# Four graph-attention layers on one core: gathers of two layers wait for earlier scores, range checks once per layer

## The chip, the cores and the metric

The kernel runs on one core of a Trainium2 chip. The metric is the device time of one execution in microseconds (us), median of several runs. A core has five engines that work side by side, each through its own queue in order: PE (TensorE, matrix products), DVE (VectorE), ACT (ScalarE), POOL (GpSimd) and SP (SyncE, which here only issues DMAs). Engines wait for each other through semaphores. An instruction whose semaphore has not been counted up yet holds everything behind it in its own queue.

## The reference, cut to what matters

```python
# x: (8, 2048, 64), adj: (2048, 2048) of 0/1, sparse
# --- layer 0 ---
h = relu(layernorm(x));  x = x + attention(h, h, adj)        # dot-product scores
# --- layer 1 ---
h = relu(layernorm(x)) @ W1
e = leaky_relu((h @ a1)[:, :, None] + (h @ a2)[:, None, :])  # additive scores
x = x + elu(softmax(where(adj > 0, e, -inf)) @ h)
# --- layer 2 ---  four heads of dot-product attention, then one more on the result
x = x + layernorm(leaky_relu(gat(leaky_relu(gat(relu(layernorm(x)), 4 heads)) @ Wo)))
# --- layer 3 ---  as layer 1 with relu for elu and weights W3
x = x + relu(softmax(...) @ h)
```

The graph is sparse, with a few nodes of high degree among the first ones. So a softmax over a row needs only the neighbours' rows, and the kernel gathers these instead of multiplying whole 2048 x 2048 matrices.

## The kernel before

**Tiles and slots.** The 2048 nodes are 16 tiles of 128. A row of a node holds all 8 batches (8 x 64 = 512 numbers). Tile i takes `ROWS[i] + PACKED[i]` slots; a slot is one gathered row for each of the 128 partitions. The tiles need 17, 8, 6, 5, 5, 5, 4, 4, 4, 4, 4, 3, 3, 3, 3, 3 slots, 81 in all, tile 0 by far the most. `gather` (L246) issues one indirect DMA per slot from POOL's queue (L253), from the layer's table in DRAM into `ring`, an SBUF buffer of 26 slots that all tiles share in turn. A slot is 2048 bytes per partition in layer 0 and layer 2, and 2080 in layers 1 and 3, whose rows carry eight additive terms (`F + B` columns).

**Stages.** `pipeline` (L214) writes the stages of all tiles one after the other: in step n it writes the last stage for tile n-s first and `take`, the gathers of the n-th tile of the layer's order, last. The program is built under `schedule_with_timeline_sim=True` (L1436): the order of instructions on each engine is fixed when the program is built, by when they become ready in a simulated time, so it isn't exactly the order of the loops.

**Layers 1 and 3** come from one function, `additive(k, ...)` (L500), with k = 1 and k = 4 (the number of the table). Its stages:

- `take`: the gathers.
- `sums` (k = 4 only): exponentials of the gathered terms (L507, ACT), their sum `S` (L510), its largest and smallest value per tile into `most` and `least` (L511, L512), an estimate `z` of the row's largest score (L515, L517), and a pair `fs`: a copy of `f1s` made on ACT (L519) and the leaky value of z (L448, called from L520).
- `first`: the scores `s` (L532, L535), leaky (L448, called from L536), the exponentials `w` (L542), copied to `wp` (L544).
- `check`: `second` (L455) adds up the weights (`by_query`, L459), inverts them (L460) and forms the weighted sum of the gathered rows: products on DVE (L380), added up on PE (L385). For k = 1 the largest and smallest `rec` per tile are noted (L550, L551).
- `third`, `project`: division (L465), transposition (L306, L307), product with the weights (L561), then `elu_add` (L567, layer 1) or `relu_add` (L905, layer 3).
- In layer 1 alone: layer norm (L267 to L298, with the power `ln_r` L290 on POOL) and `products` (L321) for layer 2.

In layer 1 POOL thus issues gathers and computes `ln_r` for tiles that are some steps further on. In layer 3 it issues gathers only.

**Range checks.** `most` and `least` hold one column per check and tile. At the end (L912 to L927) they are compared with 1e30 and 1e-30, and with other checks give `flag`; if it is set, a slow dense version runs instead. Layer 2's first attention notes `most[:, 2]` (L808), its second `most[:, 4]` in `second3` (L877, reduction L882).

Of the kernel before, what the change touches and what calls it, by code (L numbers as in the profile page):

```python
# [1 line left out]

# [6 lines left out]
F32 = mybir.dt.float32  # L9
# [4 lines left out]
OP = mybir.AluOpType  # L14
AX = mybir.AxisListType

P = 128
NEG = -1.0e30
SLOPE = 0.2
# [15 lines left out]

PAIRS = [0, 0, 2, 2, 2, 0, 0, 0, 2, 2, 2, 2, 2, 2, 2, 2]
QE = 4


MAKING = [15, 14, 13, 0, 12, 11, 10, 1, 9, 2, 8, 3, 7, 4, 6, 5]  # L40
# [19 lines left out]
def edge_stack(ctx: ExitStack, tc: tile.TileContext, x_in, adj, w1, w1t, a1, wh, wht, bh, wo, bo,  # L60
# [32 lines left out]
    mba = const.tile([P, NS], F32, name="mba")  # L93
    mbb = const.tile([P, NS], F32, name="mbb")
    nc.gpsimd.memset(mba, 0.0)
    f1s = const.tile([P, NT, B], F32, name="f1s")
    over = const.tile([P, NT, 3], F32, name="over")
    most = const.tile([P, 5, NT], F32, name="most")
    least = const.tile([P, 2, NT], F32, name="least")
    ring = const.tile([P, RING, F + B], F32, name="g")  # L100
    qidx = const.tile([P, sum(PACKED)], I32, name="qidx")
    selt_all = const.tile([P, sum(PACKED), P], F32, name="selt")
# [140 lines left out]
    def row(i, t):  # L243
        return ring[:, (held[i] + t) % RING, :F]

    def gather(k, i, st):  # L246

        n = SLOTS[i]
        assert sum(SLOTS[j] for j in held) + n <= RING
        held[i], front[0] = front[0], (front[0] + n) % RING  # L250
        cols = table[k].shape[1]
        for t in range(n):
            nc.gpsimd.indirect_dma_start(  # L253
                out=ring[:, (held[i] + t) % RING, :cols], out_offset=None, in_=table[k][:, :],
                in_offset=bass.IndirectOffsetOnAxis(ap=idx[:, OFF[i] + t:OFF[i] + t + 1], axis=0))

    def load(st, name, src, bufs):
        st[name] = rows_pool[0].tile([P, F], F32, name=name, bufs=bufs)
# [79 lines left out]
    def pre_d(k, u):  # L338

        def f(i, st):  # L340
            xh = st["xh"]
            if u is not None:
                p = ps_m.tile([P, F], F32, name="m")
                for j in range(F // P):
                    nc.tensor.matmul(p[:, 4 * j:4 * j + 4], st["xt"][:, j, :], u, start=True, stop=True)
                pv = p[:, :2 * B].rearrange("p (b t) -> p t b", t=2)
                nc.scalar.copy(f1s[:, i, :], pv[:, 0, :])
                nc.scalar.copy(xh[:, F:], pv[:, 1, :])
            store_rows(k, i, xh, k != 2)
        return f  # L350
# [94 lines left out]
            nc.vector.tensor_tensor(dst, p, u, op=OP.max)  # L445

    def leaky(dst, src):
        nc.vector.scalar_tensor_tensor(dst, src, SLOPE, src, op0=OP.mult, op1=OP.max)  # L448


    def first0(i, st):
        w = slots(w_all, i)
        exps(i, w, scores(i, st, st["rows"]), mba, D ** -0.5)

    def second(i, st, wp=None):  # L455
        w = slots(w_all, i)
        d, p = by_query(i, w, B)
        st["rec"] = small.tile([P, B], F32, name="rec")
        nc.vector.tensor_tensor(st["rec"], p, d, op=OP.add)  # L459
        nc.vector.reciprocal(st["rec"], st["rec"])  # L460
        st["y"] = weigh_sum(i, st, w) if wp is None else weigh_sum(i, st, wp, eng=nc.vector)
        done(i, st)
# [36 lines left out]

    def additive(k, wd, *finish):  # L500
        def take(i, st):
            gather(k, i, st)

        def sums(i, st):
            w = slots(w_all, i)
            for t, m, g in rows(i, 0, SLOTS[i]):
                nc.scalar.activation(w[:, t:t + m], g[:, :, F:], AF.Exp, scale=1.0 / TEMP)  # L507
            d, p = by_query(i, w, B)
            S = small.tile([P, B], F32, name="S")
            nc.vector.tensor_tensor(S, p, d, op=OP.add)  # L510
# [8 lines left out]
            nc.scalar.copy(st["fs"][:, 0, :], f1s[:, i, :])  # L519
            leaky(st["fs"][:, 1, :], z)  # L520

        def first(i, st):
            K, T = ROWS[i], PACKED[i]
            w = slots(w_all, i)
            s = slots(s_all, i)
            fs = st["fs"].rearrange("p t b -> p (t b)") if k == 4 else f1s[:, i, :]
            n = 2 * B if k == 4 else B
            pr = tiny(2 * B)
            nc.vector.tensor_copy(pr[:, :n], fs)
            pv = by_edge(i, fs, n)  # L530
            for t, m, g in rows(i, 0, K):
                nc.vector.tensor_tensor(s[:, t:t + m, :], g[:, :, F:], pr[:, None, :B].to_broadcast([P, m, B]),  # L532
                                        op=OP.add)
            for t, m, g in rows(i, K, K + T):
                nc.vector.tensor_tensor(s[:, t:t + m, :], g[:, :, F:], pv[:, t - K:t - K + m, :B], op=OP.add)  # L535
            leaky(s, s)  # L536
            if k == 4:
                nc.vector.tensor_tensor(s[:, :K, :], s[:, :K, :], pr[:, None, B:].to_broadcast([P, K, B]),
                                        op=OP.subtract)
                nc.vector.tensor_tensor(s[:, K:, :], s[:, K:, :], pv[:, :, B:], op=OP.subtract)  # L540
                nc.vector.tensor_scalar(s, s, 60.0, None, op0=OP.min)
            nc.scalar.activation(w, s, AF.Exp)  # L542
            wp = tiny((K + T) * B)
            nc.vector.tensor_copy(wp, w.rearrange("p t b -> p (t b)"))  # L544
            st["wp"] = wp.rearrange("p (t b) -> p t b", b=B)

        def check(i, st):
            second(i, st, st["wp"])
            if k == 1:
                nc.vector.tensor_reduce(most[:, 0, i:i + 1], st["rec"], AX.X, OP.max)  # L550
                nc.vector.tensor_reduce(least[:, 0, i:i + 1], st["rec"], AX.X, OP.min)  # L551
# [12 lines left out]
        mid = [sums] if k == 4 else []  # L564
        pipeline(take, *mid, first, both(check, xs_rows), third, project, *finish[1:])
# [14 lines left out]
    with tc.tile_pool(name="rows", bufs=2) as rp:  # L580
# [125 lines left out]
        with tc.tile_pool(name="more", bufs=1) as more_pool[0], psum_pools()[0] as ps_q, psum_pools()[1] as ps_t:  # L706
            bank[0] = ps_t.tile([P, F], F32, name="tiny")
            order[:] = ORDER1
            nc.sync.dma_start(out=sel_dram[:, :], in_=sel_all[0])
            additive(1, wd1, elu_add, pre_b, pre_c(q2), pre_d(2, None), products)  # L710

    with tc.tile_pool(name="l2", bufs=2) as l2p, \
# [88 lines left out]
        def second2(i, st):  # L803
            d, p = by_query(i, st["w"], B * H)
            rec = st["rec"] = small.tile([P, B, H], F32, name="rec2")
            rf = rec.rearrange("p b h -> p (b h)")
            nc.vector.scalar_tensor_tensor(rf, p, 1.0, d, op0=OP.add, op1=OP.add)
            nc.vector.tensor_reduce(most[:, 2, i:i + 1], rf, AX.X, OP.max)  # L808
# [43 lines left out]
    with psum_pools()[0] as ps_q, psum_pools()[1] as ps_t, tc.tile_pool(name="rows2", bufs=2) as rp:  # L852
# [63 lines left out]
        nc.vector.tensor_scalar(ok, most.rearrange("p k i -> p (k i)"), 1e30, None, op0=OP.is_lt)  # L916
        nc.vector.tensor_scalar(ok2, least.rearrange("p k i -> p (k i)"), 1e-30, None, op0=OP.is_gt)
# [522 lines left out]
```

## Time and profile before

| | us |
|---|---|
| median of 3 runs (lowest, highest) | 1672.45 (1670.03, 1676.54) |
| the profiled execution's own time | 1721.51 |
| its span, first to last instruction | 1719.7 |
| busy in the span: PE / DVE / ACT / POOL | 1215.1 / 1318.4 / 744.5 / 1153.4 |
| first gather of layer 1 | 402.51 |
| first gather of layer 2, first attention | 659.58 |
| first gather of layer 2, second attention | 1218.36 |
| first gather of layer 3 | 1529.04 |

By stage, in us (PE, DVE, ACT and POOL: busy time):

| stretch | length | PE | DVE | ACT | POOL | granted TensorE clock |
|---|---|---|---|---|---|---|
| layer 1, 400 to 656 | 256 | 184.81 | 181.59 | 139.71 | 107.28 | 0.89 |
| layer 2 first, 656 to 1218 | 562 | 483.48 | 434.01 | 267.40 | 459.08 | 0.95 |
| layer 2 second, 1218 to 1527 | 309 | 205.48 | 249.17 | 143.78 | 226.97 | 0.76 |
| layer 3, 1527 to 1720 | 193 | 135.70 | 102.71 | 17.92 | 76.90 | 0.83 |

A profile is one execution with a recorder running. The rows of the timeline that follow below give start, duration, engine, line, operation, output and input, shapes, count, and in brackets how long the engine sat idle before it and what ended that. "remote" and "another core or an unknown queue" stand for a semaphore that was counted up at a moment at which no recorded instruction or DMA ended; "issue" for time with no visible cause.

### The profile page before, as it was taken

What the parts mean: (1) busy time and instruction counts of PE and PEld (TensorE: products, weight loads), DVE (VectorE), ACT (ScalarE), POOL (GpSimd) and SP (SyncE); (2) the same over time, 40 slices, a digit from 0 to 9 for tenths busy, and PEclk for the clock granted to TensorE, in tenths of its full rate; (3) what the DMA queues carried; (4) which work ended last, traced back from release to release, by engine and by line L of the source; (5) the groups of instructions that cost most, each with busy time, mean ns of one, the idle gap of its engine ahead of it and who ended that gap; (6) DMA issues with size and microseconds to landing.
All of it is one profiled execution on the core that took longest, in us unless ns stands there. A gap on an engine that the chain in (4) does not pass through costs nothing.

```text
span 1719.7 us, 15784 instructions
## 1 busy us (share of the span) xinstructions
PE 1215.1 (71%) x3771; PEld 606.6 (35%) x3771; DVE 1318.4 (77%) x2748; ACT 744.5 (43%) x2378; POOL 1153.4 (67%) x903
## 2 busy tenths in 40 slices
PE   0025667776479974599997999999467877555877
PEld 0002334443234431234342444443223433333545
DVE  6979999992469987699997899831389889823656
ACT  5841324441146783356531545545234445620011
POOL 5766867786554125898789889985577896654540
PEclk9998876896699997799999999999787879657989
DMA  5555454455566447656255345200643542235651
GB/s 172 167 182 179 152 200 153 141 198 156 147 201 235 158 179 260 233 189 208 87 201 200 113 157 177 87 13 19 255 141 99 154 146 70 81 119 164 197 170 51
DMA packets 85787, 266.94 MB, mean 155 GB/s; under 512 B 14627, under 2 KB 14659, under 8 KB 75446
## 3 DMA queue, kind: packets, MB, share of 16 engines
q0 software_dynamic: 37328, 141.05, 26.7%
q1 hardware_dynamic: 48358, 124.79, 20.4%
q8 instruction: 32, 0.52, 0.1%
q14 instruction: 69, 0.57, 0.1%
HBM read 208.74 MB, written 57.05 MB: 155 GB/s over the span
## 4 chain that ended last, share of the span: by engine, by line
PE 25%; POOL 11%; DVE 9%; issue 7%; ACT 5%; DMA 3%; another core or an unknown queue 2%; DVEq 0%; SPq 0%; POOLq 0%; ACTq 0%
PE y L787 10%; PE y L385 4%; POOL g L253 3%; POOL wh L772 3%; PE m L836 2%; ACT yn L795 2%; PE m L824 2%; PE y L779 2%; POOL wg L380 1%; DMA g<-table,idx 1%; POOL ln_r L290 1%; DMA rows<-table 1%; PE m L399 1%; DVE prod L755 1%
## 5 line engine op out<-in xcount | busy, mean ns | idle before, releaser
L253 POOL DMA_INDIRECT g<-table,idx x405 | 399.2, 986 | 233.5 <-issue 161.7
L772 POOL TENSOR_TENSOR wh<-g,w 128x1024 f32<-128x1024 f32 x162 | 307.5, 1918 | 30.0 <-PE y L787 28.0
L385 PE MATMUL y<-wg,ident 128*128 128x512 f32 x392 | 234.5, 729 | 72.7 <-POOL wg L380 64.3
L290 POOL TENSOR_TENSOR ln_r<-ln_q,mhalf 128x8 f32<-128x8 f32 x80 | 135.8, 1701 | 160.6 <-DVE ln_q L288 85.1
L759 DVE TENSOR_REDUCE s<-prod 128x32 f32<-128x2048 f32 x81 | 184.0, 2286 | 14.8 <-ACT w L761 12.9
L380 POOL TENSOR_TENSOR wg<-g,w 128x1024 f32<-128x1024 f32 (+1 forms) x91 | 158.9, 1756 | 37.3 <-ACT w L436 24.2
L787 PE MATMUL y<-wh,ident 128*128 128x512 f32 x320 | 154.6, 610 | 28.9 <-POOL wh L785 25.1
L385 PE MATMUL y<-wg,selt 128*128 128x512 f32 x256 | 141.6, 663 | 5.4 <-POOL wg L380 4.4
L385 PEld LDWEIGHTS y<-wg,ident 128*128 128x128 f32 x392 | 81.6, 228 | 162.2 <-POOL wg L380 78.9
L787 PE MATMUL y<-wh,selt 128*128 128x512 f32 x256 | 124.7, 614 | 10.4 <-POOL wh L772 10.4
L795 ACT ACTIVATE yn<-y,rec 128x64 f32<-128x64 f32 x512 | 111.2, 368 | 27.5 <-PE y L787 26.9
L755 DVE TENSOR_TENSOR prod<-q,g 128x2048 f32<-128x2048 f32 x49 | 111.5, 2276 | 5.3 <-ACT g L753 4.6
L399 PE MATMUL m<-w,selt 128*128 128x8 f32 (+1 forms) x384 | 59.5, 258 | 76.0 <-ACT w L542 38.2
L380 DVE TENSOR_TENSOR wg<-g,tiny 128x1024 f32<-128x1024 f32 (+1 forms) x92 | 98.2, 1086 | 17.1 <-PE y L385 8.8
L399 PEld LDWEIGHTS m<-w,selt 128*128 128x128 f32 x384 | 63.5, 213 | 122.3 <-ACT w L542 43.6
L442 DVE SCALAR_TENSOR_TENSOR zt<-m,bhc,att 128x512 f32<-128x512 f32 x64 | 47.3, 738 | 75.0 <-ACT att L441 74.4
L298 ACT ACTIVATE xh<-x,ln_r 128x64 f32<-128x64 f32 x256 | 88.3, 428 | 18.8 <-POOL ln_r L292 18.7
L787 PEld LDWEIGHTS y<-wh,ident 128*128 128x128 f32 x320 | 59.0, 193 | 104.9 <-issue 63.8
L428 PE MATMUL q<-rows,sel 128*128 128x512 f32 x128 | 84.3, 762 | 15.7 <-DVE prod L422 5.0
L753 ACT COPY g<-g 128x512 f32<-128x512 f32 x81 | 50.4, 622 | 100.5 <-DVE prod L755 87.9
L755 DVE TENSOR_TENSOR prod<-qe,g 128x2048 f32<-128x2048 f32 x32 | 73.0, 2282 | 17.0 <-DMA qe<-qtab,qidx 15.9
L779 PE MATMUL y<-rows,ident 128*128 128x512 f32 x128 | 70.0, 634 | 18.3 <-DMA rows<-table 13.6
(210 smaller groups left out, 2584.7 us busy)
## 6 DMA issues: line engine op xcount, KB each, us to landing
qtab<-q SPq DMA_DIRECT2D x16, 1040.0 KB
a<-in_adj_dram SPq DMA_DIRECT2D x16, 1024.0 KB
q<-qtab SPq DMA_DIRECT2D x14, 1040.0 KB
table<-xh SPq DMA_DIRECT2D x48, 256.0 KB
rows<-table SPq DMA_DIRECT2D x48, 256.0 KB
xs<-x SPq DMA_DIRECT2D x48, 256.0 KB
x<-xs SPq DMA_DIRECT2D x48, 256.0 KB
table<-xh SPq DMA_DIRECT2D x32, 260.0 KB
```

What stands on the lines that cost most here:

```text
L253: nc.gpsimd.indirect_dma_start(out=ring[:, (held[i] + t) % RING, :cols], out_offset=None, in_=table[k][:, :], in_offset=bass.IndirectOffse ...
L290: nc.gpsimd.tensor_tensor(st["rstd"][:, 0, :], q, mhalf, op=OP.pow)
L298: nc.scalar.activation(dst[:, b * D:(b + 1) * D], st["src"][:, b * D:(b + 1) * D], func, bias=0.0 if st["less"] is None else r[:, 1, b:b + ...
L380: eng.tensor_tensor(wg[:, :m].rearrange("p t (b d) -> p t b d", b=B), g[:, :, :F].rearrange("p t (b d) -> p t b d", b=B), w[:, t0:t0 + m, ...
L385: nc.tensor.matmul(y, lhs(i, t), wg[:, t - t0, :], start=(t == 0 and own is None), stop=(t == n - 1))
L399: nc.tensor.matmul(p[:, :cols], selt(i, t), packed[:, t, :], start=(t == 0), stop=(t == T - 1))
L755: nc.vector.tensor_tensor(pr.rearrange("p (b h) d -> p b h d", h=H), q[:, :B * H * D].rearrange("p (b h d) -> p b h d", h=H, d=D), heads(g ...
L759: nc.vector.tensor_reduce(s[:, t - lo, :], pr, AX.X, OP.add)
L772: nc.gpsimd.tensor_tensor(wg, heads(row(i, t))[:, :, None, :].to_broadcast([P, B, 2, D]), w[:, :, 2 * k:2 * k + 2, None].to_broadcast([P, ...
L779: nc.tensor.matmul(st["ys"][j], ident, xb[:, 4 * j:4 * j + 4], start=True, stop=False)
L787: nc.tensor.matmul(st["ys"][j], lhs(i, t), wg[:, 4 * j:4 * j + 4], start=False, stop=(t == n - 1))
L795: nc.scalar.activation(yn[:, b, h, :], st["ys"][j][:, b, h, :], AF.Copy, scale=st["rec"][:, 4 * j + b, 2 * k + h:2 * k + h + 1])
```

## The change

Three edits, in the order of the title.

1. `gather` takes an instruction `behind`. In `additive`, the first gather of the n-th tile (n >= 3) gets a semaphore wait for the `leaky` of the scores (DVE) of the tile three places ahead in the order. The tile's other gathers carry no such wait themselves.
2. The reductions to `most` and `least` per tile go away in layers 1, 3 and in layer 2's second attention. The values go to `seen`, a buffer with a column per tile, which is reduced once per layer (`bounds`), over 16 x 8 columns. In layer 1 `rec` is itself a part of `seen`. `seen` is used by three layers in turn. Layer 2's first attention keeps its reduction per tile, into `most2`, and gets one more over it.
3. `f1s` gets a second place per tile for the leaky value, so the copy to `fs` on ACT (L519) goes away.

```diff
+SPREAD = 3
...
-    f1s = const.tile([P, NT, B], F32, name="f1s")
+    f1s = const.tile([P, NT, 2, B], F32, name="f1s")
     over = const.tile([P, NT, 3], F32, name="over")
-    most = const.tile([P, 5, NT], F32, name="most")
-    least = const.tile([P, 2, NT], F32, name="least")
+    most = const.tile([P, 5], F32, name="most")
+    least = const.tile([P, 2], F32, name="least")
+    seen = const.tile([P, NT, B], F32, name="seen")
+    most2 = const.tile([P, NT], F32, name="most2")
...
-    def gather(k, i, st):
+    taken = {}
+
+    def gather(k, i, st, behind=None):
...
         for t in range(n):
-            nc.gpsimd.indirect_dma_start(
+            g = nc.gpsimd.indirect_dma_start(
                 out=ring[:, (held[i] + t) % RING, :cols], out_offset=None, in_=table[k][:, :],
                 in_offset=bass.IndirectOffsetOnAxis(ap=idx[:, OFF[i] + t:OFF[i] + t + 1], axis=0))
+            if behind is not None and t == 0:
+                tc.add_manual_dep(g.ins, behind.ins.name, mybir.DependencyInfo(
+                    mybir.DependencyClass.Sync, mybir.DependencyReason.DATA), reason="gather")
...
-                nc.scalar.copy(f1s[:, i, :], pv[:, 0, :])
+                nc.scalar.copy(f1s[:, i, 0, :], pv[:, 0, :])
...
+    def bounds(at, values, low=None):
+
+        nc.vector.tensor_reduce(most[:, at:at + 1], values.rearrange("p i c -> p (i c)"), AX.X, OP.max)
+        if low is not None:
+            nc.vector.tensor_reduce(least[:, low:low + 1], values.rearrange("p i c -> p (i c)"), AX.X, OP.min)
+
-    def second(i, st, wp=None):
+    def second(i, st, wp=None, rec=None):
...
-        st["rec"] = small.tile([P, B], F32, name="rec")
+        st["rec"] = small.tile([P, B], F32, name="rec") if rec is None else rec
...
         def take(i, st):
-            gather(k, i, st)
+            n = order.index(i)
+            gather(k, i, st, taken[k, order[n - SPREAD]] if n >= SPREAD else None)
...
-            S = small.tile([P, B], F32, name="S")
+            S = seen[:, i, :]
             nc.vector.tensor_tensor(S, p, d, op=OP.add)
-            nc.vector.tensor_reduce(most[:, 1, i:i + 1], S, AX.X, OP.max)
-            nc.vector.tensor_reduce(least[:, 1, i:i + 1], S, AX.X, OP.min)
...
-            nc.vector.tensor_tensor(z, z, f1s[:, i, :], op=OP.add)
-            st["fs"] = small.tile([P, 2, B], F32, name="fs")
-            nc.scalar.copy(st["fs"][:, 0, :], f1s[:, i, :])
-            leaky(st["fs"][:, 1, :], z)
+            nc.vector.tensor_tensor(z, z, f1s[:, i, 0, :], op=OP.add)
+            leaky(f1s[:, i, 1, :], z)
...
-            leaky(s, s)
+            taken[k, i] = leaky(s, s)
...
         def check(i, st):
-            second(i, st, st["wp"])
-            if k == 1:
-                nc.vector.tensor_reduce(most[:, 0, i:i + 1], st["rec"], AX.X, OP.max)
-                nc.vector.tensor_reduce(least[:, 0, i:i + 1], st["rec"], AX.X, OP.min)
+            second(i, st, st["wp"], seen[:, i, :] if k == 1 else None)
...
             additive(1, wd1, elu_add, pre_b, pre_c(q2), pre_d(2, None), products)
+            bounds(0, seen, 0)
...
-            nc.vector.scalar_tensor_tensor(rec, p, 1.0, d, op0=OP.add, op1=OP.add)
-            nc.vector.tensor_reduce(most[:, 4, i:i + 1], rec, AX.X, OP.max)
-            nc.vector.reciprocal(rec, rec)
+            nc.vector.scalar_tensor_tensor(seen[:, i, :], p, 1.0, d, op0=OP.add, op1=OP.add)
+            nc.vector.reciprocal(rec, seen[:, i, :])
...
         pipeline(take3, first3, second3, third3, both(pre_b, xs_rows), fourth3, pre_b, pre_c(u3), pre_d(4, u3))
+        bounds(4, seen)
...
         additive(4, wd3, relu_add)
-        nc.vector.memset(most[:, 3, :], 0.0)
-        ok = small.tile([P, 5 * NT], F32, name="ok", bufs=1)
-        ok2 = small.tile([P, 2 * NT], F32, name="ok2", bufs=1)
+        bounds(1, seen, 1)
+        nc.vector.tensor_reduce(most[:, 2:3], most2, AX.X, OP.max)
+        nc.vector.memset(most[:, 3:4], 0.0)
+        ok = small.tile([P, 5], F32, name="ok", bufs=1)
+        ok2 = small.tile([P, 2], F32, name="ok2", bufs=1)
```

More of the change, by code (lines that the diff above doesn't have):

```diff
@@ L1 @@
-from contextlib import ExitStack
+from contextlib import ExitStack, nullcontext
 import concourse.bass as bass
@@ L447, in leaky @@
     def leaky(dst, src):
-        nc.vector.scalar_tensor_tensor(dst, src, SLOPE, src, op0=OP.mult, op1=OP.max)
+        return nc.vector.scalar_tensor_tensor(dst, src, SLOPE, src, op0=OP.mult, op1=OP.max)
     def first0(i, st):
@@ L525, in first @@
             s = slots(s_all, i)
-            fs = st["fs"].rearrange("p t b -> p (t b)") if k == 4 else f1s[:, i, :]
             n = 2 * B if k == 4 else B
+            fs = f1s[:, i].rearrange("p t b -> p (t b)")[:, :n]
             pr = tiny(2 * B)
@@ L807, in second2 @@
             nc.vector.scalar_tensor_tensor(rf, p, 1.0, d, op0=OP.add, op1=OP.add)
-            nc.vector.tensor_reduce(most[:, 2, i:i + 1], rf, AX.X, OP.max)
+            nc.vector.tensor_reduce(most2[:, i:i + 1], rf, AX.X, OP.max)
             nc.vector.reciprocal(rf, rf)
@@ L909, in edge_stack @@
         additive(4, wd3, relu_add)
-        nc.vector.memset(most[:, 3, :], 0.0)
-        ok = small.tile([P, 5 * NT], F32, name="ok", bufs=1)
-        ok2 = small.tile([P, 2 * NT], F32, name="ok2", bufs=1)
+        bounds(1, seen, 1)
[3 more added lines that the diff above has]
+        ok2 = small.tile([P, 2], F32, name="ok2", bufs=1)
         ok3 = small.tile([P, 3 * NT], F32, name="ok3", bufs=1)
-        nc.vector.tensor_scalar(ok, most.rearrange("p k i -> p (k i)"), 1e30, None, op0=OP.is_lt)
-        nc.vector.tensor_scalar(ok2, least.rearrange("p k i -> p (k i)"), 1e-30, None, op0=OP.is_gt)
+        nc.vector.tensor_scalar(ok, most, 1e30, None, op0=OP.is_lt)
+        nc.vector.tensor_scalar(ok2, least, 1e-30, None, op0=OP.is_gt)
         nc.vector.tensor_scalar(ok3, over.rearrange("p i k -> p (i k)"), 0.5, None, op0=OP.is_lt)
```

## The prediction

> **What bounds the kernel now.** I read the page's groups first, then the busy time in stretches of 20 us over layer 1, then the timelines of POOL, DVE and ACT there, and the same for layer 3. The change acts in layers 1 and 3, and a little in layer 2's second attention, so the rest (layer 0 and layer 2's first attention, 960 us) is taken as it is.
>
> Windows of layer 1; columns are the stretch, its length, busy time (and count) of PE, PEld, DVE, ACT and POOL, granted clock, DMA share and GB/s:
>
> ```profile
> 400.00:420.00 20.00, 10.10 (x26) 5.57 (x26) 8.33 (x32) 0.67 (x3) 13.35 (x14) 0.57 0.58 165
> 420.00:440.00 20.00, 5.22 (x26) 3.05 (x24) 2.60 (x11) 0.59 (x1) 15.18 (x16) 0.77 0.75 213
> 440.00:460.00 20.00, 7.48 (x26) 5.36 (x26) 6.97 (x19) 5.42 (x15) 7.59 (x8) 0.54 0.48 132
> ...
> 560.00:580.00 20.00, 19.70 (x74) 10.34 (x74) 20.00 (x42) 16.58 (x47) 1.93 (x3) 1.00 0.35 133
> ```
>
> From about 500 on DVE is the bound (20.00 of 20). From 420 to 460 nothing works but POOL. There it issues gathers one after another, 1.25 us apart (0.95 each and 0.30 between), 35 of them without a break. Timelines of POOL, ACT and DVE:
>
> ```profile
> 445.20 0.95 POOL L253 DMA_INDIRECT g<-table,idx  x1 [0.30 <-issue]
> 455.21 0.95 POOL L253 DMA_INDIRECT g<-table,idx  x1 [9.06 <-DVE wg L380]
> 462.15 1.68 POOL L290 TENSOR_TENSOR ln_r<-ln_q,mhalf 128x8 f32<-128x8 f32 x1 [3.49 <-DVE ln_q L288]
> ```
> ```profile
> 451.10 0.60 ACT L570 ACTIVATE e<-q 128x512 f32<-128x512 f32 x1 [29.48 <-remote]
> ```
> ```profile
> 434.30 0.17 DVE L535 TENSOR_TENSOR s<-g,m 128x16 f32<-128x16 f32 x1 [8.21 <-remote]
> 452.39 0.70 DVE L572 SCALAR_TENSOR_TENSOR q<-q,e 128x512 f32<-128x512 f32 x1 [17.38 <-ACT e L571]
> ```
>
> ACT waits 29.48 us for the product q of L561, which PE started at 421.66 and whose recorded end is 422.83. PE's count was seen only at 451.07, with three later ones within 0.2 us. So PE's work was done and its count held back, a *hole*. The gathers' packets dry up at 449.5: the hole ends as the run of gathers ends. Layer 3 shows the same: gathers from 1529.04 to 1568.95 without a break, packets dry at 1572, and
>
> ```profile
> 1573.45 0.69 DVE L906 SCALAR_TENSOR_TENSOR x<-q,x 128x512 f32<-128x512 f32 x1 [13.32 <-remote]
> 1598.99 0.69 DVE L465 TENSOR_TENSOR att<-y,rec 128x512 f32<-128x512 f32 x1 [3.69 <-remote]
> ```
>
> Idle DVE time in these holes: layer 1: 8.21 + 16.1 (435.0 to 451.1) + 5.2 (att, 492.27) = 29.5 us; layer 3: 7.4 (1558.09) + 13.3 + 3.7 + 5.6 (1634.40, "unknown queue" in the chain) = 30.0. Together 59.5 us.
>
> **Which time the sum is made against.** The profiled execution took 1721.51 us, 49.1 more than the median 1672.45. That is nearly the holes' 59.5. [...] By the rows alone the holes are time to be won, up to 59.5 us; [...] a timed run has only 59.5 - 49.1 = 10.4 us of them. No row shows which. I take the second because of the match of the two sums: PE alone is held back, and only after some 18 us of gathers in a row. So I work in differences and subtract them from 1672.45.
>
> **Part 1, the wait.** It adds no instruction, only 13 waits per layer, on POOL for DVE. Does it bind? I laid each tile's first gather beside the leaky of three tiles before, counting gathers in tile order. In layer 1 the leakies of tiles 1 to 3 of the order ran at 409.10, 413.42 and 418.46; the gathers of tiles 4 to 6 began at 413.87, 417.63 and 421.38, some 3 to 5 us later. So the first 19 gathers aren't moved. Tile 7 (17 slots) began at 426.39, its gate is at 434.83: held 8.4 us, by the hole itself. Later tiles of layer 1 are held 10.5 to 24.9 us, but their scores ran 39 to 51 us after their last gather, and a gather needs 3.8 us from issue to use (405.11 to L535 at 408.90). So this costs nothing: DVE's backlog of earlier tiles hides it, and if that were gone the cost would be the excess over some 35 us of lead, none here. In layer 3 the tightest is tile 7 again: held 28.5 us (1555.46 to 1584.01), then 17 x 1.25 + 3.8 = 25.1 us, ready at 1609.1 against scores at 1612.10. Covered by 3.0 us.
>
> Behind the waiting gather in POOL's queue stand, in layer 3, only gathers. In layer 1 they are also `ln_r` (1.65 us each), for which ACT's xh (L298), PE's transposes, and all of `products` wait. Before, all but three of the gathers of tiles up to the seventh are ahead of the first `ln_r` at 462.15, which itself waited for DVE (3.49), so there the queue took little. Without the hole that `ln_r` would have been ready some 25 us earlier and have stood behind gathers until 450; the wait can only put some behind it. Gain of the order change between 0 and 10 us in a timed run; the near row is the 3.49 us wait, which says 0. I take 0. SP's loads and stores stay where they are, since none of them depends on a gather.
>
> The holes: with the wait, a hole stops itself. Leaky doesn't come, POOL stops, packets dry up, PE's counts come through. The first 19 gathers take 24 us and already touch a hole; after that the runs are 17 at most by gate, where 35 and 32 stood. About half of a timed run's 10.4 us might go; between 0 and 10.4. I take 3.
>
> **Part 2, the checks.** Timeline of DVE in layer 1:
>
> ```profile
> 413.28 0.15 DVE L550 TENSOR_REDUCE most<-rec 128x1 f32<-128x8 f32 x1
> 413.35 0.15 DVE L551 TENSOR_REDUCE least<-rec 128x1 f32<-128x8 f32 x1
> 413.42 0.17 DVE L448 SCALAR_TENSOR_TENSOR s<-s 128x24 f32<-128x24 f32 x1
> ```
>
> 0.15 us each, but the next starts 0.07 later, so a reduction costs 0.075 of DVE. Layer 1: 32 go; those where DVE is full (ten tiles of 16): 20 x 0.075 = 1.5 us. Layer 2's second attention: 16 x 0.075 = 1.2, half of it in a stretch with DVE at 0.8: 0.6. Layer 3: both stand between S (L510) and z (L515), on the way to the scores, 16 x 0.15 = 2.4 us; DVE is half idle there (102.71 of 193), so only that dependency counts, and I take all of it. Added: five or six reductions over 128 or 16 columns. The nearest row is 0.23 us for 80 columns (1702.59), so some 0.3 each; two fall where DVE waits for the next table (8.69 us before the copy at 399.73 is such a wait), the last on the flag, which was ready at 1709.57, 4.6 us ahead of the last x at 1714.19. Nothing.
>
> **Part 3, the copy.** 16 x 0.197 us of ACT, which is nearly idle in layer 3 (17.92 of 193). But the copy waits for a free fs buffer at the head of ACT's queue, with exponentials behind it:
>
> ```profile
> 1588.94 0.20 ACT L519 COPY fs<-f1s 128x8 f32<-128x8 f32 x1 [3.57 <-DVE tiny L529]
> ```
>
> Such waits outside holes: 2.33 + 4.95 + 3.57 + 0.88 = 11.7 us. The group of waits puts 5.2 us of PE's weight loads (L399) on this copy. Between 0 (something else is late) and 11.7; I take 3, about half of PE's share: what is late next is the exponential's own gather or PE's queue.
>
> Sum: 3 + 1.5 + 0.6 + 2.4 + 3 = 10.5 us. 1672.45 - 10.5 = **1662**. The profiled execution should fall by more: 7.5 for parts 2 and 3 and half of the 59.5, to about 1684.
>
> **Rivals.**
> - *The holes are real and close* (the wait does what its place suggests in timed runs too). For it: they end exactly as packets do, and nothing proves that recording makes them. Against: the match of 59.5 with 49.1. Half of 59.5 plus 7.5: 1672.45 - 37 = 1635.
> - *A gather waiting at the head of POOL's queue holds `ln_r` back* (slower). In layer 1 between 490 and 560 six tiles' gathers would be held. The waits for a free ring slot show one such hold: 9.06, 6.75, 2.10 and 4.62, mean 5.6; six are 34 us. DVE's backlog covers about one tile's pace, 10 us; it decides once DVE runs out of products. 34 - 10 - 7.5 = +16.5: 1689. Against it: the order is laid out by readiness with the wait known, so `ln_r` can stand ahead of the held gather.
> - *The wait doesn't do what it says.* Only a tile's first gather carries it. The others are ready at once, and DVE's queue shows readiness before program order (at 409.86 both wg of L380 run ahead of L459, written before them). If these go ahead, runs stay as long and parts 2 and 3 vanish among other waits: 1671.
>
> **How the numbers follow.** Forecast (1656 to 1668) 0.52, holes real (1628 to 1650) 0.23, POOL held (1680 to 1698) 0.15, no effect 0.10. The span that holds 8 in 10 goes from 1638 to 1686; the forecast's own range is narrower. What can be told from no change is 0.5%, 8.4 us: faster means under 1664.1. Of the forecast's 0.52 some 0.33 lies below that and 0.19 within; so faster 0.33 + 0.23 = 0.56, same 0.19 + 0.10 + 0.01 = 0.30, slower 0.14.
>
> **What would show it.** In the profile after: runs of more than 20 gathers in a row are gone in layers 1 and 3 (wait works) or not (it doesn't); "remote" waits of ACT and DVE shrink well below 59.5 us while the median falls by much less (holes are the recorder's), or by as much (they are real); `ln_r` with waits of 5 us behind a gather that waits for L448 (POOL held); exponentials of layer 3 no longer behind a copy. A median under 1650 or over 1680 would make the forecast wrong.

## The result, and the profile after

The changed kernel takes 1662.06 us (median of 6 runs, 1659.44 to 1662.88) against 1673.39 for the kernel before (6 runs on the same chip), a ratio of 0.9929 with a 95% interval of 0.9914 to 0.9944: 11 to 12 us less. The forecast was 1662. Its sum came out for other reasons than it gave, as the runs below show.

The page of the changed kernel, its first lines and its two groups of POOL:

```profile
span 1660.9 us, 15702 instructions
...
PE 1214.6 (73%) x3771; PEld 606.7 (37%) x3771; DVE 1311.9 (79%) x2674; ACT 741.6 (45%) x2362; POOL 1151.1 (69%) x903
...
L259 POOL DMA_INDIRECT g<-table,idx x405 | 396.2, 978 | 222.4 <-issue 131.7
...
L299 POOL TENSOR_TENSOR ln_r<-ln_q,mhalf 128x8 f32<-128x8 f32 x80 | 135.9, 1702 | 129.0 <-DVE ln_q L297 93.0
```

The recorded execution took 1662.6, as long as the timed ones. That of the kernel before had taken 49 us more than its timed ones. The same stretches of layer 1 show why (the stretch, its length, busy time and count of PE, PEld, DVE, ACT and POOL, granted clock, DMA share, GB/s):

```profile
400.00:420.00 20.00, 10.21 (x23) 4.74 (x23) 7.21 (x25) 0.68 (x4) 11.70 (x13) 0.57 0.55 158
420.00:440.00 20.00, 13.60 (x56) 8.70 (x55) 11.16 (x32) 8.03 (x24) 15.12 (x17) 0.77 0.79 230
440.00:460.00 20.00, 15.37 (x60) 10.19 (x60) 11.53 (x30) 0.99 (x5) 16.25 (x16) 0.84 0.65 186
560.00:580.00 20.00, 18.42 (x69) 9.55 (x68) 20.00 (x46) 16.55 (x48) 3.52 (x4) 1.00 0.45 173
```

From 420 to 460 DVE now works 22.7 of 40 us, where it had 9.6, and PE 29.0 where it had 12.7. No wait of the trace ends on "remote" any more: the holes are gone. But POOL still issues 35 gathers in a row at the start of the layer. So the wait hadn't done what the holes were said to need, and the first question was whether the wait had closed the holes at all.

Stages are read from the trace in one way throughout: from one table's first gather to the next one's (the 81st, 162nd and so on of the 405), and the last to the end. A stage is read from one recorded execution per kernel, and timed executions of one kernel differ by up to 15 us (the kernel before from 1664.7 to 1680.3). So a stage's difference counts only where whole groups of kernels agree in it.

| profile of | layer 1 | layer 2, first attention | layer 2, second | layer 3 |
|---|---|---|---|---|
| before | 257.1 | 558.8 | 310.7 | 190.6 |
| after | 231.5 | 557.7 | 308.1 | 158.9 |

### The profile page after: what moved, and what is told of

Same layout as the page of the kernel before. It is cut to its first block, busy times and chain, and to the rows that moved or that the text cites. A ratio compares the mean times of both kernels' runs of the same rounds, so it can differ in the third digit from the quotient of the medians.

```text
span 1660.9 us, 15702 instructions
## 1 busy us (share of the span) xinstructions
PE 1214.6 (73%) x3771; PEld 606.7 (37%) x3771; DVE 1311.9 (79%) x2674; ACT 741.6 (45%) x2362; POOL 1151.1 (69%) x903
## 5 line engine op out<-in xcount | busy, mean ns | idle before, releaser
L797 PE MATMUL y<-wh,selt 128*128 128x512 f32 x256 | 124.6, 613 | 10.4 <-POOL wh L782 10.4
L389 DVE TENSOR_TENSOR wg<-g,tiny 128x1024 f32<-128x1024 f32 (+1 forms) x92 | 98.1, 1086 | 12.3 <-PE y L394 11.9
L315 PE MATMUL q<-ident,xh 128*128 128x128 f32 x192 | 51.3, 341 | 44.9 <-ACT xh L307 43.1
```

What stands on the lines that cost most here:

```text
L389: eng.tensor_tensor(wg[:, :m].rearrange("p t (b d) -> p t b d", b=B), g[:, :, :F].rearrange("p t (b d) -> p t b d", b=B), w[:, t0:t0 + m, ...
L797: nc.tensor.matmul(st["ys"][j], lhs(i, t), wg[:, 4 * j:4 * j + 4], start=False, stop=(t == n - 1))
```

## The experiments

Each was timed in five rounds beside the kernel before on the same chip. The first eight ran on one chip, where the kernel before takes 1672.5 us; the next three on a second (1725.7), the last on a third (1722.5). Diffs are against the kernel that is named.

**The kernel before, again**, with no edit.

> The kernel before, unchanged, run as an experiment. Theory (the holes, in which counts of TensorE come late, are a fluke of one profiled execution): ratio 1.000 within 0.3%, and the profiled execution of this run takes about 1672 us, not 1721, without waits marked remote of more than 2 us in layers 1 and 3. Rival (every recorded execution of the kernel before has the holes, because of its long runs of gathers): profiled time again some 40 to 50 us above the median, with remote waits of 20 us and more in layer 1.

1672.54 (ratio 1.0005, 0.9995 to 1.0015), and its recorded execution 1674.0, with no wait on "remote". Layer 1 took 235.9 us and layer 3 163.2, without any edit. Its stretches of layer 1 beside those above:

```profile
420.00:440.00 20.00, 17.27 (x71) 10.32 (x72) 17.02 (x62) 8.71 (x27) 15.14 (x16) 0.89 0.83 237
440.00:460.00 20.00, 11.91 (x47) 8.47 (x47) 7.69 (x20) 0.32 (x1) 16.17 (x16) 0.76 0.68 196
```

POOL's column is as full of gathers as in the first profile, and DVE and PE work beside it. So the holes don't come with every execution, and the change didn't close any here: this trace, and not the first, is what the changed kernel is compared with below. Layer 1 then fell by 4.4 us and layer 3 by 4.2. (What the holes are is told with the last four runs.)

**The wait alone**, on the kernel before (the edits of `gather` and `leaky` are the change's own and left out here):

```diff
-            gather(k, i, st)
+            n = order.index(i)
+            gather(k, i, st, taken[k, order[n - 3]] if n >= 3 else None)
```

> The kernel before with the wait of the first gather of each tile alone; checks and copy as before. Theory (the sum of the prediction): 3 us less than before, ratio 0.998. Rival 1 (the wait brings all of it): 0.993. Rival 2 (the wait binds nowhere, since a tile's other gathers go ahead): 1.000, with 35 or more gathers in a row in layer 1 as before.

1666.72, ratio 0.9962 (0.9947 to 0.9977): 6 us. Layer 1 took 231.0 us, as with the whole change.

**The change without its wait**, so the checks and the copy:

```diff
-            gather(k, i, st, taken[k, order[n - SPREAD]] if n >= SPREAD else None)
+            gather(k, i, st, None)
```

> The changed kernel without the wait: checks once per layer and no copy. Theory (the sum): 7.5 us less than before, ratio 0.9955. Rival 1 (the wait brings all of it): 1.000. Rival 2 (the wait binds nowhere): 0.993, the same as the changed kernel.

1673.45, ratio 1.000 (0.9985 to 1.0014): nothing, where 7.5 us were forecast for these parts. Layer 1 is back at 236.1. So 6 and 0 make 12, and something is missing from one of them.

**The wait on every gather of a tile**, on the changed kernel:

```diff
-            if behind is not None and t == 0:
+            if behind is not None:
```

> The changed kernel with the wait on every gather of a tile, not on its first alone. Theory (scores run 20 us and more after their gathers, so holding gathers costs nothing): same as the changed kernel, ratio to before 0.993, last gathers of layers 1 and 3 later by 10 to 20 us. Rival (a gather at the head of POOL's queue holds the power of the layer norm back): layer 1 longer by 5 us or more, ratio 0.997 or above.

1689.94, ratio 1.0105 (1.0089 to 1.0121): 18 us slower than before. This run turned out to be the one that says most about layer 1. Timeline of POOL in the kernel before (its second profile), in the changed kernel and in this one; layer 1 starts at 406.2, 404.6 and 405.8:

```profile
453.54 1.68 POOL L290 TENSOR_TENSOR ln_r<-ln_q,mhalf 128x8 f32<-128x8 f32 x1
...
465.62 0.22 POOL L292 TENSOR_TENSOR ln_r<-ln_m,ln_r 128x8 f32<-128x8 f32 x1
...
470.79 0.21 POOL L292 TENSOR_TENSOR ln_r<-ln_m,ln_r 128x8 f32<-128x8 f32 x1
```
```profile
448.20 1.69 POOL L299 TENSOR_TENSOR ln_r<-ln_q,mhalf 128x8 f32<-128x8 f32 x1
...
461.54 0.21 POOL L301 TENSOR_TENSOR ln_r<-ln_m,ln_r 128x8 f32<-128x8 f32 x1
...
464.18 0.22 POOL L301 TENSOR_TENSOR ln_r<-ln_m,ln_r 128x8 f32<-128x8 f32 x1
```
```profile
453.06 1.69 POOL L299 TENSOR_TENSOR ln_r<-ln_q,mhalf 128x8 f32<-128x8 f32 x1
...
465.15 0.21 POOL L301 TENSOR_TENSOR ln_r<-ln_m,ln_r 128x8 f32<-128x8 f32 x1
...
470.32 0.21 POOL L301 TENSOR_TENSOR ln_r<-ln_m,ln_r 128x8 f32<-128x8 f32 x1
```

None of these waits for anything: each stands in the queue behind gathers, and has no idle time before it. What the first `ln_r` needs had long been there. DVE's timeline in the kernel before (second profile):

```profile
434.77 0.16 DVE L288 TENSOR_SCALAR ln_q<-ln_q 128x8 f32<-128x8 f32 x1
```

This `ln_q` was ready at 434.93, so the first `ln_r` lost 18.6 us to the gathers ahead of it. ACT's `xh` needs the second half, the product of L292 or L301. ACT's timeline in the kernel before and in the changed one:

```profile
465.88 2.76 ACT L298 ACTIVATE xh<-x,ln_r 128x64 f32<-128x64 f32 x8 [10.41 <-POOL ln_r L292]
```
```profile
461.78 4.42 ACT L307 ACTIVATE xh<-x,ln_r 128x64 f32<-128x64 f32 x13 [6.95 <-POOL ln_r L301]
```

In the changed kernel three gathers fewer (35, not 38) stand ahead of the first `ln_r`. Later gathers and products are dealt out differently too. This is order and not waiting: no gather of the changed kernel is held back for scores in the first 97 us of the layer. The first one that is:

```profile
502.69 0.95 POOL L259 DMA_INDIRECT g<-table,idx  x1 [0.84 <-DVE s L457]
```

Over the nine profiles without holes the start of layer 1 goes by these places:

| kernels | first ln_r | first product | second product | layer 1 |
|---|---|---|---|---|
| before again; change without wait; wait in layer 3 alone (below) | +47.3 | +59.4 | +64.6 | 235.9, 236.1, 234.4 |
| wait on every gather | +47.3 | +59.4 | +64.5 | 236.0 |
| after; wait alone; wait in layer 1; two more below | +43.6 | +56.9 | +59.5 | 231.5, 231.0, 229.0, 231.5, 229.9 |

(us from the layer's first gather.) The kernel that holds back most gathers has its first two `ln_r` and their products where the kernel without a wait has them, and layer 1 takes as long. So it doesn't look like the holding back that wins there, but like the place of `ln_r` in POOL's queue: a second product 5.0 us earlier, a layer 4.9 us shorter (230.6 against 235.5 on average). DVE's order isn't what decides. It differs in some 70 places within the first row and within the last, between kernels with and without checks per tile, and the layer's length doesn't follow it. But ACT's and PE's orders differ between the rows too, and no run without holes moved `ln_r` alone, so the place of `ln_r` is the likely cause and not a proven one.

Layer 3 shows what holding back costs. Waits in layer 3 of this kernel, and of the changed one (us in total, times, longest):

```profile
ACT w L523 <- DMA g<-table,idx: 95.2, 19, 16.3
...
POOL g L259 <- DVE s L457: 18.8, 4, 8.3
```
```profile
ACT w L523 <- DMA g<-table,idx: 81.1, 17, 14.2
...
POOL g L259 <- DVE s L457: 8.3, 2, 8.0
```

POOL waits 10 us longer for scores, and the exponentials wait 14 us longer for gathers; the layer takes 170.0 us against 158.9. Of the 27 us between the two profiles 11 are here, 4.5 in layer 1, 3 and 7 in layer 2's first and second attention, to which the next runs come.

**The wait in one layer only**, on the changed kernel; first layer 1, then layer 3:

```diff
-            gather(k, i, st, taken[k, order[n - SPREAD]] if n >= SPREAD else None)
+            gather(k, i, st, taken[k, order[n - SPREAD]] if n >= SPREAD and k == 1 else None)
```
```diff
+            gather(k, i, st, taken[k, order[n - SPREAD]] if n >= SPREAD and k == 4 else None)
```

> The changed kernel with the wait in layer 1 alone. Theory A (the wait wins in both layers, by two different ways): layer 1 gives the 4.5 us seen between the stages of the wait kernel and the kernel without it, layer 3 nothing here, so 1673 - 5 = 1668, ratio 0.997, and the layer 3 stage stays near 164 us. Rival B (all of the gain is layer 1's, and the shorter layer 3 in the profile of the changed kernel is chance): 1662, ratio 0.993, as with the whole change. Rival C (layer 1's wait counts only because layer 3's follows): 1673, ratio 1.000.

> The changed kernel with the wait in layer 3 alone. Theory A: layer 1 as without a wait (236 us), layer 3 some 4 to 5 us shorter (159 us): 1668, ratio 0.997. Rival B: 1673, ratio 1.000, layer 3 at 164 us.

Layer 1 alone: 1664.88, ratio 0.9955 (0.9938 to 0.9971), layer 3 at 162.1. Layer 3 alone: 1669.86, ratio 0.9983 (0.9970 to 0.9995), layer 1 at 234.4, layer 3 at 162.1. Both bring something, so B and C fall. But layer 1 brings 7.5 us against the kernel without a wait, not the 4.5 to 5 that its stage shows.

**The wait with the checks**, and **the wait with the copy taken out**. The first is the changed kernel with `fs` and its copy put back (the line that reads `fs` is left out here):

```diff
+            st["fs"] = small.tile([P, 2, B], F32, name="fs")
+            nc.scalar.copy(st["fs"][:, 0, :], f1s[:, i, 0, :])
-            leaky(f1s[:, i, 1, :], z)
+            leaky(st["fs"][:, 1, :], z)
```

The second is the kernel before with the change's edits of `take`, `gather`, `leaky` and `f1s`, and the reductions as they were.

> The changed kernel with the copy of the attention terms put back (waits in both layers, checks once per layer). The wait alone gave 1667 and the whole change 1662; checks and copy without a wait gave nothing. Theory A1 (the copy is what stands on the path in layer 3 once the gathers wait, as it heads ACT's queue): as the wait alone, 1667, ratio 0.996. Theory A2 (the two reductions between the sum S and the scores are what counts): 1662, ratio 0.993. Half each: 1664.5.

> The kernel before with the wait in both layers and without the copy, the checks per tile kept. Theory A1 (the copy counts): 1662, ratio 0.993. Theory A2 (the reductions count): 1667, ratio 0.996. Together with the run beside it the two should share the 5 us between the wait alone and the whole change.

With the checks 1661.58, ratio 0.9944 (0.9925 to 0.9962); with the copy out 1667.74, ratio 0.9967 (0.9955 to 0.9979). By these the checks bring all that is left and the copy nothing. Yet the checks had brought nothing without the wait. The answer lies in layer 2's first attention, where the change does no more than give a reduction another place to write to. The length of that stage in all nine profiles without holes:

| order of ACT's instructions in that stage | kernels | us |
|---|---|---|
| as in the kernel before | before again, after, wait in layer 1, wait and checks | 558.4, 557.7, 557.7, 557.5 |
| 28 stretches of it differ | wait alone, without wait, wait on every gather, wait in layer 3, wait and copy | 561.7, 562.3, 561.0, 561.8, 560.9 |

Either of two edits in layer 1, the wait or the once-per-layer checks, lays out layer 2's first attention in the second order; both together, or neither, in the first. (The wait on every gather is an exception: it has both and the second order.) The orders of PE, DVE and POOL change with ACT's, and each row has kernels with and without each part of the change. So the second order is what costs 3.7 us (561.5 against 557.8). With that taken off where it applies, the parts come near to adding up, in us against the kernel before:

| kernel | by its ratio | without the other order |
|---|---|---|
| checks and copy, no wait | 0.0 | -3.7 |
| wait alone | -6.4 | -10.1 |
| wait and checks, copy kept | -9.4 | -9.4 |
| wait and no copy, checks per tile | -5.5 | -9.2 |
| wait in layer 1, checks and copy | -7.5 | -7.5 |
| wait in layer 3, checks and copy | -2.8 | -6.5 |
| the whole change | -11.9 | -11.9 |

Layer 1's wait is then worth 4 to 5 us (7.5 less 3.7; 11.9 less 6.5), layer 3's 3 to 4 (6.5 less 3.7; 11.9 less 7.5), checks and copy together 2 to 4. Each ratio carries some 2.5 us of interval. So layer 3's share is barely clear of it, and checks and copy can't be split: the wait with one of them (9.4, 9.2) shows no more than the wait alone (10.1).

**Layer 1's checks put back tile by tile**, on the kernel without the wait, to test the order: one edit that adds work and brings the first order back. (Left out here: `bounds(0, ...)` goes, and two reductions over the 16 columns of `mx1` and `mn1` come at the end.)

```diff
-            second(i, st, st["wp"], seen[:, i, :] if k == 1 else None)
+            second(i, st, st["wp"])
+            if k == 1:
+                nc.vector.tensor_reduce(mx1[:, i:i + 1], st["rec"], AX.X, OP.max)
+                nc.vector.tensor_reduce(mn1[:, i:i + 1], st["rec"], AX.X, OP.min)
```

> The kernel without the wait (1673.5), with layer 1's 32 small reductions put back tile by tile. Its instructions in layer 2's first attention, which no edit touches, stand in the order of the kernel before again, and not in that of the kernel without the wait. Theory (the laid-out order of that attention is worth some 4 us, and hid what the checks and the copy bring): that stage goes from 562 to 558 us, and though DVE has more to do in layer 1 the time falls to 1669.5, ratio 0.998. Rival (a check costs what its instructions cost, the order nothing): 1.5 us back, 1675, ratio 1.001.

**ln_r ahead of gathers, by order alone**, on the kernel without the wait; and the same, earlier still, on the changed kernel. `normed[0]` is the first tile's `ln_r` product, and the edge is marked `NoSync`: it sets an order within POOL's queue and no semaphore. The edit names the slots one by one; written short:

```diff
+            if k == 1 and order.index(i) == 6 and t >= 10:
+                tc.add_manual_dep(g.ins, normed[0].ins.name, mybir.DependencyInfo(
+                    mybir.DependencyClass.NoSync, mybir.DependencyReason.DATA), reason="norm")
```

> The kernel without the wait; in layer 1 the gathers from the seventh tile's eleventh slot on stand behind the first tile's ln_r and its product in POOL's queue, by order alone, with no semaphore. 31 gathers then stand ahead of the first ln_r where 38 stood, 36 ahead of its product where 45 stood. Layer 2's first attention has the order of the kernel before. Theory (the wait wins in layer 1 because ln_r moves up past gathers): layer 1 falls from 236 to 231 us or less (227 at best), layer 2's first attention 558: 1673.5 - 4 - 5 = 1664.5, down to 1660, ratio 0.993 to 0.995. Rival (the wait wins by what it holds back, not by the order of ln_r): layer 1 stays at 236, 1669.5, ratio 0.998.

> The changed kernel with the same ordering from the seventh tile's seventh slot on: 25 gathers ahead of the first ln_r where 35 stood, 26 ahead of its product where 43 stood. Theory: ln_q is ready 32 us into the layer, as 25 gathers end, so ln_r comes some 11 us earlier than in the changed kernel and layer 1 falls by 5 to 10 us to 222 to 227: 1652 to 1657, ratio 0.988 to 0.991 (layer 2's first attention has a third order here, which can add or take some 4 us). Rival (from here DVE's own work is the bound of layer 1): 1662, ratio 0.993. Rival (the held gathers make the seventh tile late): over 1664.

These three came to the second chip, and there everything is some 50 us longer: the kernel before takes 1725.65 (30 executions, 1717.96 to 1735.33). That is what its first profile had shown (1721.5), and the holes are back. ACT's timeline in the run with layer 1's checks put back:

```profile
456.88 0.60 ACT L584 ACTIVATE e<-q 128x512 f32<-128x512 f32 x1 [29.57 <-remote]
...
498.45 0.60 ACT L584 ACTIVATE e<-q 128x512 f32<-128x512 f32 x1 [15.10 <-remote]
```

These are the two waits of the first profile, 29.48 and 14.95, to a tenth or two. Layer 1 took 257.8 us and layer 3 187.1.

*Checks of layer 1 back*: ratio 0.9981 (0.9968 to 0.9994), layer 2's first attention 559.2. The theory said 0.998, the rival 1.001. Work was added to the kernel that had gained nothing, and it gains 3 us. But the kernel without the wait wasn't run on this chip, and the two ratios, 0.9981 and 1.000, overlap in their intervals. What the trace shows by itself is the first order, with a stage as long as in the first profile (558.8). The absolute 1669.5 of the theory meant the first chip and can't be compared.

*ln_r by order, no wait*: 1712.34, ratio 0.9918 (0.9892 to 0.9944), layer 1 246.8, which is 11.0 us less than in the run beside it. ACT's timeline:

```profile
448.26 0.60 ACT L588 ACTIVATE e<-q 128x512 f32<-128x512 f32 x1 [23.30 <-remote]
...
468.57 2.76 ACT L311 ACTIVATE xh<-x,ln_r 128x64 f32<-128x64 f32 x8 [6.69 <-POOL ln_r L304]
```

The first product came 60.4 us into the layer, against 72.2 in the run with the checks put back. So layer 1 is won with no gather waiting for scores, and by more than the theory's 5. But the holes shrank with it: ACT's first wait is 6 us shorter, and the second (15.10) isn't there. POOL's run of gathers had stopped earlier, before the 30th, for products of DVE:

```profile
452.37 0.95 POOL L259 DMA_INDIRECT g<-table,idx  x1 [8.28 <-DVE wg L398]
```

On this chip the place of `ln_r` and the shorter holes can't be told apart.

*The wait, and ln_r earlier still*: 1712.59, ratio 0.9923 (0.9897 to 0.9949), layer 1 247.8. The first product came at +44.3, but the second only at +68.8, and the layer is no shorter for it. The theory's 0.988 to 0.991 missed. Here the change's own wait stopped a run of gathers, for `leaky` (L466), and the hole was the shortest of all. ACT's and POOL's timelines:

```profile
437.31 0.60 ACT L588 ACTIVATE e<-q 128x512 f32<-128x512 f32 x1 [12.77 <-remote]
```
```profile
441.90 0.95 POOL L259 DMA_INDIRECT g<-table,idx  x1 [8.08 <-DVE s L466]
```

Whether this kernel would beat the changed one on the first chip wasn't seen.

**The order once more**, on the kernel without the wait, with nearly the dose that the wait gives: edges for the seventh tile from slot 15 on and the eighth to `normed[0]`, for the first three slots of the ninth to `normed[1]`.

> The kernel without the wait; the last gathers of the seventh tile (from its sixteenth slot on) and those of the eighth stand behind the first tile's ln_r and its product in POOL's queue, and the first three of the ninth behind the second tile's: by order alone, no gather waits for scores. 34 gathers stand ahead of the first ln_r and 36 ahead of its product, where the wait has 35 and 43, and the kernel without it 38 and 45. Layer 2's first attention has the order of the kernel before. On a chip where PE's counts come through (before at 1673): theory (the wait wins in layer 1 by the place of ln_r) layer 1 at 231 us or less, layer 2's first attention 558: 1664.5, ratio 0.995. Rival (it wins by what it holds back): layer 1 at 236, 1669.5, ratio 0.998. On a chip where counts are held back while gathers run (before at 1726): theory layer 1 some 5 to 10 us under 257, ratio 0.992 to 0.995; rival 257, ratio 0.998.

This one came to the third chip, which has the holes too (before 1722.47): 1714.99, ratio 0.9956 (0.9937 to 0.9975). Layer 1 took 255.0 us, 2.8 less than with the checks put back on the second chip and 2.1 less than in the first profile, where the theory asked for 5 to 10. Here `ln_r` was bounded from the other side: it waited 15.23 us for `ln_q`, which the hole had held up, and the second product came at +75.1 against +77.4: 2.3 earlier for 2.8 of the layer. The whole gain is 7.6 us, of which some 3 are checks and copy; the rest, some 2 us, isn't accounted for. The run fits the place of `ln_r` in direction and not in size.

## Why the prediction came out right, step by step

The sum was 10.5 us: holes 3, checks 4.5, copy 3. Measured were 11 to 12, of which the wait 8 to 10 and the rest 2 to 4. The wait was put too low and the rest too high, by about the same; that they cancel is luck.

- **Which time to work from: wrong.** The prediction gave the 59.5 us of holes to the recording, and left 10.4 for timed runs. That was its author's estimate, from 59.5 being near the 49.1 between the profile and the median. The runs refute that: unrecorded executions of the kernel before take 1725.7 on one chip with the holes, and a recorded one takes 1674.0 on a chip without. The profile and the median simply came from two conditions. That recording holds PE back, no run here shows: on the first chip 1674.0 recorded stands beside 1672.5 timed, and that recorded execution has no holes. So the 3 us taken for them don't exist. To subtract differences from 1672.45 and not from 1721.5 was still the right choice, but by luck: the reason for it wasn't seen.
- **The order of POOL, "between 0 and 10, I take 0": the term that was mis-sized.** It is some 5 us in layer 1, as far as the runs single it out. The step went wrong by reading the nearest row, a 3.49 us wait of `ln_r` for DVE, in an execution where a hole had made DVE late. Without holes `ln_q` is there 18.6 us before `ln_r` runs. The prediction had written the right sentence (`ln_r` would "have stood behind gathers") and then thought that a wait could only put more in front of it. Here the dependency moved gathers back in the order in which the program is laid out, and `ln_r` moved up: 35 gathers stand ahead of the first one, where 38 had stood.
- **"The wait costs nothing" in layer 3, covered by 3.0 us: right in that it costs nothing.** By the totals of two pairs of runs it even wins 3 to 4 us there, each with an interval about as large. The stage itself says less: 2.3 and 3.1 us shorter in these pairs, but 163.7 with the wait alone against 163.2 in the kernel before. So the gain is likely and not shown, and how it comes about is open. ACT's wait for transposed tiles is 41.3, 50.8 and 44.9 us in the three runs without a wait in layer 3 and 31.6 to 37.5 in the six with one, but the orders of all engines differ too. That the cover is thin is shown by the wait on every gather, which loses 11 us.
- **The checks, 4.5, and the copy, 3: too large.** Together 2 to 4. For the copy the waits show where part of the rest went. ACT's waits in layer 3, of the kernel before (second profile) and after:

```profile
ACT xt L307 <- PE q L306: 41.3, 13, 5.9
ACT fs L519 <- PE m L412: 9.7, 4, 4.1
ACT w L542 <- DVE z L517: 5.8, 1, 5.8
ACT fs L519 <- DVE tiny L529: 4.6, 2, 3.6
ACT w L542 <- DVE s L541: 3.7, 4, 1.1
```
```profile
ACT xt L316 <- PE q L315: 37.3, 12, 5.9
ACT w L554 <- DVE s L553: 16.8, 8, 4.9
```

  The 14.3 us of waits at the copy are gone, and the exponential of the scores (L542 before, L554 after), next in ACT's queue, waits 16.8 us for DVE where it had waited 9.5. About half of the wait was handed on, which is what the lower end of the prediction's bound was about.
- **The rivals.** *The wait doesn't do what it says* was right in its mechanism: other gathers of a tile go ahead of the first one (as the program is laid out, the seventh tile's first gather is the 34th of layer 1, behind fifteen of its others), and runs of 35 remain, so the sign named for "the wait works" didn't come. Its 1671 was wrong, since the order shifts all the same. *A held gather holds `ln_r` back* is hardly seen with one gated gather per tile: three `ln_r` stand right behind a held gather, and run 0.5 to 0.7 us after their `ln_q` is ready. With all gated the kernel is indeed slower, at 1690 against the rival's 1689, but by its stages through layer 3's late gathers and longer attentions in layer 2, and not through `ln_r` behind a held gather, which stood where it does without a wait. *The holes are real*: they are, on two of three chips, but not where the forecast was timed. What the change itself makes of them wasn't tried. The wait with `ln_r` moved up gained 13 us of 1726 there and shortened ACT's 29.5 us wait to 12.8, in the order that the prediction described: POOL stopped for `leaky` at +29.9, and the wait ended at +33.4.
- **What no step foresaw** is the 3.7 us that an untouched stage gains or loses by its laid-out order. In the whole change two shifts of order cancel. Had only one of them come, it would have been 1666.

## What to carry to other kernels

Before you use a profile to explain a time, see that the two belong together: a recorded span 3% from the timed median is a question to settle first, by recording again, and not one to explain by the recorder. When the program is laid out by readiness, a new dependency is also a new order: look in each queue for what now stands earlier or later, above all for small instructions behind long runs of others, as `ln_r` here, which stood behind 38 gathers of 1.25 us and came to stand behind 35. And when parts of a change don't add up, compare the stages that none of them touches.

## What the runs showed of the hardware

PE's counts came late while POOL issued gathers in all four runs on the second and third chip (ACT's longest wait on "remote" in layer 1: 29.57, 23.30, 12.77 and 30.16 us) and in none of the eight on the first. Before's two profiles have the same instructions in layer 1 and nearly the same run of gathers. In one, ACT waited 29.48 us for a product whose record had ended 28 us earlier (where a product ends is modelled in the trace, but PE started its next ten between 422.66 and 425.83, 25 us before the wait ended); in the other there is no such wait. The timed executions are longer on the second and third chip too, by 53 and 50 us: the kernel before takes 1725.65 and 1722.47 there, where the first chip has 1672.5.

What stood behind a waiting instruction in an engine's queue waited with it. In the first profile the scores of a tile's `w` were there at 435.00, and `w` ran at 452.26, behind the `e` that had waited until 451.10. Timelines of DVE and ACT:

```profile
434.83 0.17 DVE L448 SCALAR_TENSOR_TENSOR s<-s 128x24 f32<-128x24 f32 x1
```
```profile
452.26 0.21 ACT L542 ACTIVATE w<-s 128x24 f32<-128x24 f32 x1
```

The long hole of layer 1 ended 3.5 to 5 us after POOL's first run of gathers stopped, in all five profiles that have one, though POOL stopped for different things (us from the layer's first gather):

| profile of | POOL stops issuing | because the next one waits for | ACT's long wait ends | later by |
|---|---|---|---|---|
| before, first profile | +43.6 | DVE's products `wg` | +48.6 | 4.9 |
| checks of layer 1 back | +43.7 | DVE's products `wg` | +48.7 | 5.0 |
| `ln_r` by order | +36.2 | DVE's products `wg` | +40.3 | 4.2 |
| wait, and `ln_r` earlier | +29.9 | DVE's `leaky`, the change's wait | +33.4 | 3.5 |
| order once more | +42.3 | DVE's `ln_q`, for `ln_r` | +47.1 | 4.8 |

In the first profile the last packet of these gathers ended at 448.6 (the prediction read 449.5), 2.5 us before the hole did. Not every count waits for the stop: DVE's wait of 8.21 us in that profile ended at +31.8, in the middle of the run. What holds the counts isn't known, nor whether POOL's issuing or the packets matter. And since the last four runs came later, but the first profile came before all, whether it is the chip or something else at work on it at the time isn't told apart.
